# Logit columns as stationary weights in layer 1, six buffers for the softmax rows, a later flag transpose, and one product on VectorE: one change to a four-layer graph kernel

## The chip, the cores and the metric

The kernel runs on one core of a Trainium2 chip. The metric is the device time of one execution in microseconds (us). Each kernel is timed in several executions, and the median counts. A separate execution is recorded by the hardware profiler, and everything said of single instructions comes from that one.

## What is computed

`x` holds 2708 nodes of 256 features and `adj` is a 2708 x 2708 weighted adjacency matrix, which is non-negative in these inputs. Four layers follow one another, each with a residual and a layer norm:

```
x = _layernorm(x + _L0_gnn_ref(x, adj, L0_gnn_W), axis=-1)
x = _layernorm(x + _L1_gnn_ref(x, adj, L1_gnn_W, L1_gnn_a, L1_gnn_gamma, L1_gnn_beta), axis=-1)
x = _layernorm(x + _L2_gnn_ref(x, adj, adj, ...), axis=-1)
x = _layernorm(x + _L3_gnn_ref(x, adj, L3_gnn_neigh_W, L3_gnn_lin_W), axis=-1)
```

Layer 0 is `A @ (x * W)`. Layer 1 is graph attention with 4 heads of 64 features, and a layer norm of its own. Layer 2 needs a sum over neighbours that goes through a GRU cell (the "edge" cell), and graph attention with K = 3 heads, whose logits start from one column per head for every node, `u = x @ (gat_W[k] @ gat_a[k])`; its result goes through a second GRU cell (the "node" cell). Layer 3 is `adj @ h / degree` and a projection.

## The kernel before

**Tiles.** The nodes are 22 tiles of 128 (the last has 20). They are put in six groups (`spans`) of 4, 4, 4, 4, 3 and 3 tiles, and layer 1 works on two groups at a time: `for g in range(0, len(spans), 2)` at L801 gives g = 0, 2 and 4, 8 tiles, 8 tiles and 6.

**Layer 1.** For each g there are two passes (q = 0 and 1), one for each pair of heads. A pass runs over the 22 source tiles c in blocks of two: VectorE builds the unnormalised attention `p` (L855), TensorE multiplies it into `acc` (`heads`, L831: weights 64 columns wide, two products beside each other in the array) and into the sums `den` (`totals`, L841: weights 32 columns wide, four beside each other). The f32 products are recorded as two matmuls each ("passes" of a product below; x counts in the profile count them).

**What is woven in.** `step(c)` at L809 runs after each source tile. It ends the 8 tiles of the previous g in four pairs: `layer1_end` (L697) turns the sums, divides, applies layer 1's norm and the outer norm; `layer1_logits` (L762) then turns the finished `xs` (L770), copies the result into `turn` (L772), writes it to DRAM (L780), and multiplies it with `uw`, the three columns `gat_W[k] @ gat_a[k]`: here the 128 x 128 piece of x is the stationary operand and `uw` the moving one, 3 columns wide (L788). ScalarE copies the 3 columns of both tiles to `u_all` (L792). The pairs of g = 4 have no later pass to hide in; they are run in `while turns` (L907 to L913), between pieces of `raw_sums` (`next(ahead)`).

**The outer norm.** Its last step (L757, L758) is on ScalarE: the negative mean times the reciprocal deviation `rs2`, then a scaled copy into `xs`. `rs2` is a power taken by GpSimd (`power`, L694).

**raw_sums and seven.** `raw_sums` (L365) computes the neighbour sums for the edge cell in six stretches r, each of 11 steps c. A step loads four blocks of `adj_t` (`pa`, issued on SP, L275), clears the own block on GpSimd (L286), forms three sums on VectorE and changes one block in place (L315 to L318), and feeds seven products (L328): the first two use the loaded blocks as they are, the others the sums.

**The logits and the softmax rows of layer 2.** After all pairs are done, `u_all` is split into three bf16 parts (L920) and multiplied with the mask (L932). Later each node has two numbers per head (`st`: a shift and a reciprocal). L1054 to L1071 turn them into rows: six transposes into `ps_t` (L1060), a ScalarE copy into `sr` (L1064), which has two buffers, and DMAs on GpSimd's queue into `st_d` (L1070).

**The flag.** `most` (L1075) is the largest negative part of `adj` per partition. It is turned by TensorE (L1077), reduced to one number (L1079) and made an integer (L1081), which selects a slow path at the very end when an entry is negative. The transpose takes a PSUM tile of the pool `ps_t`; after that the pools are closed (L1117), and the edge cells `gru_t` (L1084) take the same banks as `ps_g`.

**The edge cells.** L1126 to L1139: for each r, the x columns are loaded (SP, L257), the raw sums are run to one stretch ahead, and for r below 4 `gru_t` does 24 gate products (L1097), evacuated by ScalarE (L1102, L1111) and finished on VectorE (L1109 to L1115). The main loop of layer 2 (L1358) starts behind this; `load_stats` (L1160, SP, DMA at L1166) reads the softmax rows of its first unit, ScalarE makes p from them (L1369, L1372) and VectorE multiplies by the blocks (L1373).

**What sets the order.** The program gives a priority by the order in which it is written; a scheduler then orders each engine's instructions by when their inputs are expected. [...]A change in one place can move instructions of other lines past each other.

Of the kernel before, what the change touches and what calls it, by code (L numbers as in the profile page):

```python
# [19 lines left out]
P = 128  # L20
# [7 lines left out]
def kernel(  # L28
# [351 lines left out]
                edges.append(y)  # L380
            yield

    uw = const.tile([P, FC, K], F32, name="uw")

    lwn_d = dram.tile([P, FC, 2 * F], F32, name="lwn_d")

# [22 lines left out]
    if True:  # L409
# [12 lines left out]
        if True:  # L422
# [252 lines left out]
            if True:  # L675
# [21 lines left out]
                def layer1_end(pool, pair):  # L697
# [56 lines left out]
                    for i, (t, s, sums, dens, row) in enumerate(pair):  # L754
                        n = sz(t)
                        o = turn[:, row * F : (row + 1) * F]
                        nc.scalar.mul(mean2[:n, i : i + 1], mean2[:n, i : i + 1], rs2[:n, i : i + 1])  # L757
# [4 lines left out]
                def layer1_logits(pair, apart=1):  # L762

                    pt = ps_t.tile([P, 4, P], F32, tag="tr", name="tr")
                    at = (2 * GT + 1 + 2 * (pair[0][-1] // 2 % 2)) * F
                    xt = turn[:, at : at + 2 * F].rearrange("p (i f n) -> p i f n", i=2, f=FC)
                    for i, a in enumerate(pair):
                        t, n = a[0], sz(a[0])
                        for f in range(FC):
                            nc.tensor.transpose(pt[:, i * FC + f, :n], xs[t][:n, f * P : (f + 1) * P], ident[:n, :n])  # L770
                    if all(sz(a[0]) == P for a in pair):
                        nc.scalar.copy(xt.rearrange("p i f n -> p (i f) n"), pt)  # L772
                    else:
                        for i, a in enumerate(pair):
                            n = sz(a[0])
                            nc.scalar.copy(xt[:, i, :, :n], pt[:, i * FC : (i + 1) * FC, :n])
                    for i, a in enumerate(pair):
                        t, n = a[0], sz(a[0])
                        at, _, d = [p for p in xt_d if p[0] <= t * P][-1]
                        nc.gpsimd.dma_start(d[:, :, t * P - at : t * P - at + n], xt[:, i, :, :n])  # L780
                    for _ in range(apart):
                        yield

                    pm = ps_t.tile([P, 4, P], F32, tag="tr", name="pm")
                    for i, a in enumerate(pair):
                        n = sz(a[0])
                        for f in range(FC):
                            nc.tensor.matmul(  # L788
                                pm[:n, i, :K], xt[:, i, f, :n], uw[:, f, :], start=(f == 0), stop=(f == FC - 1)
                            )  # L790
# [7 lines left out]
                ended = []  # L798

                dens = [keepr.tile([P, W], F32, name=f"den{s}") for s in range(2)]  # L800
                for g in range(0, len(spans), 2):  # L801
# [7 lines left out]
                    def step(c):  # L809
                        with tc.issue_after(product.ins) if g == 0 else nullcontext():  # L810
                            for s in list(steps):
                                if next(s, s) is s:
                                    steps.remove(s)

                        if q == 0 and c % 5 == 1 and len(halves) < len(ended):
                            halves.append(layer1_end(l1, ended[len(halves)]))
                            next(halves[-1])
                            steps.append(itertools.islice(halves[-1], 2))

                        if q == 1 and c % 5 == 0 and c // 5 < len(halves):  # L820
                            steps.append(itertools.chain(halves[c // 5], [None], layer1_logits(ended[c // 5], 1 + (g + 2 >= len(spans)))))
                            next(steps[-1])

                    for q in range(H // 2):
# [82 lines left out]
                while turns:  # L907
                    for a in turns[: k + 1]:
                        if next(a, a) is a:
                            turns.remove(a)  # L910
                            k -= 1
                    next(ahead)
                    k += 1  # L913

                u_parts = sums_pool.tile([P, NT, CT], BF16, name="u_parts", bufs=1)
# [135 lines left out]
                drows = tail.tile([NT, P], F32, name="drows", bufs=1)  # L1051
                nc.scalar.copy(drows, pt[:NT, 0, :])
                nc.gpsimd.dma_start(diag_d, drows)
                for lo in range(0, NT, 4):  # L1054
                    hi = min(lo + 4, NT)
                    at, w = lo * P, width(lo, hi)
                    pt = ps_t.tile([P, 4, P], F32, tag="tr", name="pst")
                    for t in range(lo, hi):
                        n = sz(t)
                        nc.tensor.transpose(  # L1060
                            pt[: 2 * K, t - lo, :n], st[:n, t].rearrange("p i k -> p (i k)"), ident[:n, :n]
                        )
                    sr = tail.tile([2 * K, W], F32, tag="sr", name="sr")
                    nc.scalar.copy(sr[:, :w], pt.rearrange("p t n -> p (t n)")[: 2 * K, :w])  # L1064
                    for u, (a, uw_) in enumerate(units):
                        for h in range(2):
                            c0, c1 = max(at, h * NH + a), min(at + w, h * NH + a + uw_)
                            if c0 < c1:
                                off = c0 - h * NH - a
                                nc.gpsimd.dma_start(st_d[u][:, h, off : off + c1 - c0], sr[:, c0 - at : c1 - at])  # L1070
                    next(ahead)  # L1071
# [7 lines left out]
            nc.vector.tensor_reduce(one, pt[:1, 0, :], AX.X, ALU.max)  # L1079
# [41 lines left out]
    with pool("e_in") as e_in, pool("e_work") as ework, pool("ps_g", 4, space=PSUM, side="right") as ps_g:  # L1121
# [4 lines left out]
        for r, (a, w) in enumerate(raws):  # L1126
# [621 lines left out]
```

## Time and profile before

| what | us |
| --- | --- |
| median of 3 runs | 1837.92 |
| lowest, highest | 1837.21, 1839.69 |
| the profiled execution | 1839.03 |
| its span, first to last instruction | 1837.3 |
| TensorE matmuls busy | 1818.2 |
| VectorE busy | 1265.9 |
| ScalarE busy | 699.5 |
| GpSimd busy | 294.6 |

The mean granted clock of TensorE is 0.999. In the profile, PE is TensorE's matmuls, PEld its weight loads, DVE VectorE, ACT ScalarE, POOL GpSimd and SP SyncE; SPq or ACTq is an engine's queue of DMA issues. A line of the timeline gives the start, the length, the engine, the line of the kernel, the operation, what is written and read, the number of merged instructions (x), and in brackets how long the engine had been idle and what ended that. Layer 0 lasts to about 242 us, layer 1's passes to about 578, the `while turns` stretch to about 617, the softmax rows and the flag to about 694, the edge cells to about 870; the rest is layer 2's main loop and layer 3.

### The profile page before, as it was taken

How to read it: one execution, taken by the hardware profiler on the slowest of the kernel's cores; microseconds unless marked ns; L12 is line 12 of the kernel's file. 1: busy time of each engine (PE TensorE's matmuls, PEld its weight loads, DVE VectorE, ACT ScalarE, POOL GpSimd, SP SyncE). 2: the span in 40 equal slices, each digit the busy share in tenths (PEclk: the TensorE clock that was granted, in tenths of full speed). 3: DMA queues.
4: the chain of work that ended last, by engine and by line, in shares of the span. 5: the costliest groups of instructions: out<-in, count | busy, mean ns of one | idle time of the engine just before them, and what ended most of it. 6: DMA issues, size and time to landing. Idle time of an engine off the chain costs nothing.

```text
span 1837.3 us, 23072 instructions
## 1 busy us (share of the span) xinstructions
PE 1818.2 (99%) x7512; PEld 1037.5 (56%) x7512; DVE 1265.9 (69%) x2242; ACT 699.5 (38%) x1449; POOL 294.6 (16%) x441
## 2 busy tenths in 40 slices
PE   9999999999999999999999999999999999999998
PEld 7888842233446886888444444444445556655556
DVE  5333399999797656554658888686887768945664
ACT  3444420023145114111555655555654656321011
POOL 1322221011113501000002000110300202021211
PEclk9999999999999999999999999999999999999999
DMA  9343310000113567654657666453555445634764
GB/s 303 116 157 138 127 54 25 24 1 21 33 28 95 125 159 189 169 133 106 177 140 203 183 170 173 125 151 110 169 161 129 120 114 142 181 90 122 205 168 134
DMA packets 435710, 237.32 MB, mean 129 GB/s; under 512 B 184460, under 2 KB 422445, under 8 KB 433149
## 3 DMA queue, kind: packets, MB, share of 16 engines
q1 hardware_dynamic: 423534, 210.76, 42.1%
q0 software_dynamic: 7696, 20.50, 3.4%
q10 hardware_dynamic: 4350, 4.50, 0.7%
q8 instruction: 62, 1.02, 0.2%
q14 instruction: 68, 0.55, 0.1%
HBM read 223.00 MB, written 12.66 MB: 128 GB/s over the span
## 4 chain that ended last, share of the span: by engine, by line
PE 89%; DMA 4%; ACT 2%; issue 1%; DVE 1%; SPq 1%; POOL 1%; POOLq 0%; DVEq 0%; ACTq 0%
PE m L328 41%; PE acc L831 11%; PE acc L214 8%; PE bank L1228 8%; PE den L841 6%; PE bank L1204 3%; PE gate L1097 3%; PE bank L1271 2%; PE acc L528 2%; PE pm L434 1%; DMA strip<-in_adj_t_dram 1%; PE m L1475 1%; PE pq L1018 1%; SPq L275 1%; ACT p L1369 1%
## 5 line engine op out<-in xcount | busy, mean ns | idle before, releaser
L855 DVE SCALAR_TENSOR_TENSOR p<-fall,rise,mask 128x1024 f32<-128x1024 f32 (+1 forms) x264 | 288.9, 1154 | 24.3 <-PE den L841 17.0
L1369 ACT ACTIVATE p<-st,e_neg 128x1024 f32<-128x1024 f32 (+1 forms) x198 | 197.4, 1040 | 194.2 <-PE m L328 188.4
L328 PE MATMUL m<-s,xq 128*128 128x512 f32 (+3 forms) x660 | 230.2, 467 | 0.0
L831 PE MATMUL acc<-p,h 128*64 128x512 f32 (+2 forms) x1056 | 209.2, 546 | 0.0
L214 PE MATMUL acc<-turn,strip 128*128 128x257 f32 x792 | 182.7, 381 | 0.9 <-DMA strip<-in_adj_t_dram 0.7
L315 DVE TENSOR_TENSOR s<-p 128x512 f32<-128x512 f32 (+3 forms) x132 | 81.2, 616 | 148.6 <-PE m L328 112.8
L328 PE MATMUL m<-p,xq 128*128 128x512 f32 (+1 forms) x396 | 183.0, 544 | 0.1
L1372 ACT ACTIVATE p<-p 128x1024 f32<-128x1024 f32 (+1 forms) x198 | 178.9, 943 | 0.2
L328 PE MATMUL m<-p,x 128*128 128x512 f32 (+1 forms) x396 | 167.7, 542 | 0.3 <-DVE supt L345 0.3
L328 PEld LDWEIGHTS m<-s,xq 128*128 128x128 f32 x660 | 124.3, 190 | 76.3 <-issue 59.5
L1373 DVE TENSOR_TENSOR p<-p,blk 128x1024 f32<-128x1024 f32 (+1 forms) x132 | 143.0, 1103 | 29.0 <-ACT p L1372 12.5
L214 PEld LDWEIGHTS acc<-turn,strip 128*128 128x128 f32 x792 | 147.2, 189 | 23.1 <-DMA strip<-in_adj_t_dram 2.7
L831 PEld LDWEIGHTS acc<-p,h 128*64 128x64 f32 x1056 | 72.1, 137 | 128.4 <-issue 120.7
L328 PE MATMUL m<-s,x 128*128 128x512 f32 (+3 forms) x330 | 127.2, 467 | 0.0
L328 PEld LDWEIGHTS m<-p,xq 128*128 128x128 f32 x396 | 74.6, 190 | 76.9 <-issue 61.3
L328 PEld LDWEIGHTS m<-p,x 128*128 128x128 f32 x396 | 74.9, 190 | 75.4 <-issue 60.9
L466 DVE TENSOR_SCALAR mask<-strip 128x2816 fp8e4<-128x2816 f32 (+5 forms) x40 | 39.0, 1003 | 110.3 <-DMA strip<-in_adj_t_dram 110.1
L841 PE MATMUL den<-p,h 128*32 128x512 f32 (+2 forms) x1056 | 110.4, 546 | 0.0
L286 POOL TENSOR_TENSOR blk<-blk,offdiag 128x128 f32<-128x128 f32 (+3 forms) x50 | 30.0, 605 | 357.2 <-DMA blk<-in_adj_t_dram 313.4
L481 ACT ACTIVATE below<-strip 128x384 bf16<-128x384 f32 x132 | 78.3, 594 | 18.1 <-DMA strip<-in_adj_t_dram 14.7
L328 PEld LDWEIGHTS m<-s,x 128*128 128x128 f32 x330 | 62.0, 190 | 39.2 <-issue 34.6
L316 DVE TENSOR_TENSOR p<-p 128x512 f32<-128x512 f32 (+3 forms) x132 | 81.6, 618 | 2.4
(295 smaller groups left out, 2647.1 us busy)
## 6 DMA issues: line engine op xcount, KB each, us to landing
strip<-in_adj_t_dram SPq DMA_DIRECT2D x19, 1408.0 KB, 6.1
blk<-in_adj_t_dram SPq DMA_DIRECT2D x88, 256.0 KB, 3.5
blk<-in_adj_t_dram SPq DMA_DIRECT2D x88, 192.0 KB, 4.1
turn<-in_adj_t_dram SPq DMA_DIRECT2D x44, 256.0 KB, 3.2
pa<-in_adj_t_dram SPq DMA_DIRECT2D x88, 128.0 KB, 2.6
blk<-in_adj_t_dram SPq DMA_DIRECT2D x88, 128.0 KB, 2.5
p<-in_adj_t_dram SPq DMA_DIRECT2D x88, 128.0 KB, 2.7
turn<-in_adj_t_dram SPq DMA_DIRECT2D x44, 192.0 KB, 3.2
```

The costliest lines, as they stand in the source:

```text
L214: at = nc.tensor.matmul(acc, s[:, c, :n], rhs(c), start=(c == 0), stop=(c == NT - 1))
L315: nc.vector.tensor_tensor(s1, a21, a22, ALU.add)
L316: nc.vector.tensor_tensor(a21, a21, a11, ALU.subtract)
L328: nc.tensor.matmul(dst[:, :w], lt, rt, start=start and not (one_bank and i in (3, 4, 6)), stop=stop and not (one_bank and i in (1, 2, 5)))
L481: nc.scalar.activation(below[:, : (hi - lo) * P], s[:, lo:hi].rearrange("p c n -> p (c n)"), AF.Relu, scale=-1.0, accum_out=negative[:, BE ...
L831: at = nc.tensor.matmul(acc[s][i * HD : (i + 1) * HD, :ws], hs[c][:, 2 * q + i, :HD], ps[i][:, p0 : p0 + ws], **flags,)
L841: at = nc.tensor.matmul(den[j : j + CT, :ws], hs[c][:, 2 * q + i, HD + 1 - CT :], ps[i][:, p0 : p0 + ws], **flags,)
L855: nc.vector.scalar_tensor_tensor(p[:, :w], fall_b[:, i, :w], rise[:, c, 2 * q + i : 2 * q + i + 1], mask[:, c, at : at + w], ALU.max, ALU. ...
L1228: nc.tensor.matmul(g[:, :w], lt, rt, start=(q == 0), stop=(q == len(terms) - 1))
L1369: nc.scalar.activation(p[:, :, :w], st_k[:, :, :w], AF.Relu, scale=-1.0, bias=e_neg[:, at, k : k + 1])
L1372: nc.scalar.activation(p[:, :, :w], p[:, :, :w], AF.Exp, scale=-1.0)
L1373: nc.vector.tensor_tensor(p[:, :, :w], p[:, :, :w], blk[:, i, :, :w], ALU.mult)
```

## The change

Five edits:

1. `uw` becomes 32 columns wide, filled with zeros beyond the three. In g = 2 and 4 the pairs' logits take `uw` as the stationary operand and the turned x of both tiles as the moving one, 256 columns, so that pair number `slot` writes 32 partitions of its own; ScalarE copies those 32 x 256 numbers to a row of `turn`. When all four pairs are done, `logit_rows` turns the 128 x 256 block back with two transposes and copies it to `u_all` in one instruction. It runs at c = 3 of the next g's first pass, or, for the last, behind the first `next(ahead)` in `while turns`. The pairs of g = 4 keep the old form.
2. In g = 4 the fourth pair's products come one step sooner than the other three.
3. For the last pair the product of mean and `rs2` is on VectorE instead of ScalarE.
4. The six softmax rows are copied into six buffers: the four `sum` tiles and two `den` tiles of layer 1 in place of two of the pool `tail`.
5. The flag's transpose, reduction and comparison stand behind the first edge cell's `gru_t` and use a bank of `ps_g`.

```diff
-    uw = const.tile([P, FC, K], F32, name="uw")
+    uw = const.tile([P, FC, CT], F32, name="uw")
+    nc.gpsimd.memset(uw, 0.0)
...
-                        nc.scalar.mul(mean2[:n, i : i + 1], mean2[:n, i : i + 1], rs2[:n, i : i + 1])
+                        if pair[-1][0] == NT - 1:
+                            nc.vector.tensor_tensor(mean2[:n, i : i + 1], mean2[:n, i : i + 1], rs2[:n, i : i + 1], ALU.mult)
+                        else:
+                            nc.scalar.mul(mean2[:n, i : i + 1], mean2[:n, i : i + 1], rs2[:n, i : i + 1])
...
                     pm = ps_t.tile([P, 4, P], F32, tag="tr", name="pm")
+                    if slot is not None:
+                        rows = slice(slot * CT, (slot + 1) * CT)
+                        at = (14 + pair[0][0] // (2 * GT) % 2) * F
+                        lines = turn[:, at : at + 2 * P].rearrange("p (i n) -> p i n", i=2)
+                        for f in range(FC):
+                            nc.tensor.matmul(
+                                pm[rows, :2], uw[:, f], xt[:, :, f, :], start=(f == 0), stop=(f == FC - 1)
+                            )
+                        nc.scalar.copy(lines[rows], pm[rows, :2])
+                        if slot + 1 == len(pairs):
+                            pending.append(pairs)
+                        return
...
+                def logit_rows(pairs):
+
+                    full, t = len(pairs) * CT, pairs[0][0][0]
+                    at = (14 + t // (2 * GT) % 2) * F
+                    pt = ps_t.tile([P, 4, P], F32, tag="tr", name="pu")
+                    for i in range(2):
+                        nc.tensor.transpose(pt[:, i, :full], turn[:full, at + i * P : at + (i + 1) * P], ident[:full, :full])
+                    nc.scalar.copy(
+                        u_all[:, t : t + 2 * len(pairs)].rearrange("p (j i) k -> p i j k", i=2),
+                        pt[:, :2, :full].rearrange("p i (j s) -> p i j s", s=CT)[:, :, :, :K],
+                    )
...
+                        if q == 0 and c == 3 and pending:
+                            logit_rows(pending.pop())
...
-layer1_logits(ended[c // 5], 1 + (g + 2 >= len(spans)))))
+layer1_logits(ended[c // 5], 1 + (g + 2 >= len(spans) and c < 15), c // 5, ended)))
...
                     next(ahead)
+                    if pending:
+                        logit_rows(pending.pop())
...
+                rows = [keepr.tile([P, W], F32, tag=f"sum{i // 2}{i % 2}", name="sr") for i in range(4)] + dens
...
-                    sr = tail.tile([2 * K, W], F32, tag="sr", name="sr")
+                    sr = rows.pop(0)[: 2 * K]
...
-            pt = ps_t.tile([P, 4, P], F32, tag="tr", name="pl")
-            nc.tensor.transpose(pt[:1, 0, :], most, ident)
-            one = const.tile([1, 1], F32, name="one")
-            nc.vector.tensor_reduce(one, pt[:1, 0, :], AX.X, ALU.max)
-            signed = const.tile([1, 1], I32, name="signed")
-            nc.vector.tensor_scalar(signed, one, 0.0, None, ALU.is_gt)
...
                 gru_t(ps_g, ework, yt, edges[r], xt, 2 * w, wih, whh, b_edge)
+                if r == 0:
+                    pt = ps_g.tile([P, W], F32, tag="gate", name="pl")
+                    nc.tensor.transpose(pt[:1, :P], most, ident)
+                    one = const.tile([1, 1], F32, name="one")
+                    nc.vector.tensor_reduce(one, pt[:1, :P], AX.X, ALU.max)
+                    signed = const.tile([1, 1], I32, name="signed")
+                    nc.vector.tensor_scalar(signed, one, 0.0, None, ALU.is_gt)
```

The order of the instructions, laid beside that of before, changes as follows. TensorE: only the lists named above, and two products of `raw_sums` (L328) that stood between the flag's transpose and the first gate product come behind the gate products of the first edge cell and the flag. SP: the x columns of the second edge cell come nine issues sooner, and the load of the first softmax rows (L1166) comes behind 21 more issues for `pa`. ScalarE: the first p of layer 2 (L1369) comes behind the first four evacuations of the first edge cell instead of ahead of them. VectorE: the second step of `raw_sums` behind the softmax rows comes wholly ahead of the first p product (L1373), and ahead of the third step there are two p products instead of four, and two half-width sums of p (L315 to L318) instead of seven. In the passes of g = 4 small instructions of ScalarE and VectorE (L685 to L748) change places among each other.

More of the change, by code (lines that the diff above doesn't have):

```diff
@@ L760, in layer1_end, with layer1_logits @@
                         )
-                def layer1_logits(pair, apart=1):
+                def layer1_logits(pair, apart=1, slot=None, pairs=()):
                     pt = ps_t.tile([P, 4, P], F32, tag="tr", name="tr")
@@ L788, in layer1_logits @@
                             nc.tensor.matmul(
-                                pm[:n, i, :K], xt[:, i, f, :n], uw[:, f, :], start=(f == 0), stop=(f == FC - 1)
+                                pm[:n, i, :K], xt[:, i, f, :n], uw[:, f, :K], start=(f == 0), stop=(f == FC - 1)
                             )
@@ L796, in layer1_logits @@
                             nc.scalar.copy(u_all[:n, a[0]], pm[:n, i, :K])
-                ended = []
+                def logit_rows(pairs):
[8 more added lines that the diff above has]
+                    )
+                ended, pending = [], []
                 dens = [keepr.tile([P, W], F32, name=f"den{s}") for s in range(2)]
@@ L820, in step @@
                         if q == 1 and c % 5 == 0 and c // 5 < len(halves):
-                            steps.append(itertools.chain(halves[c // 5], [None], layer1_logits(ended[c // 5], 1 + (g + 2 >= len(spans)))))
+                            steps.append(itertools.chain(halves[c // 5], [None], layer1_logits(ended[c // 5], 1 + (g + 2 >= len(spans) and c < 15), c // 5, ended)))
                             next(steps[-1])
```

## Prediction

> **What bounds the kernel now.** I read the page's part 1 and chain first, then the busy time of each engine in stretches of 10 us, then the timeline wherever TensorE falls short of 10.
>
> ```profile
> PE 1818.2 (99%) x7512; PEld 1037.5 (56%) x7512; DVE 1265.9 (69%) x2242; ACT 699.5 (38%) x1449; POOL 294.6 (16%) x441
> ...
> PE 89%; DMA 4%; ACT 2%; issue 1%; DVE 1%; SPq 1%; POOL 1%; POOLq 0%; DVEq 0%; ACTq 0%
> ```
>
> TensorE is the bound; only what shortens its list or closes one of its gaps counts. The span has 1837.3 - 1818.2 = 19.1 us of gaps, and the change can reach few of them. Near an edited line TensorE falls short in three places: by 0.98 us in 600 to 610, by 0.88 in 690 to 700, and by 0.67 and 0.33 in 710 to 720 and 720 to 730, where VectorE is busy 9.97 and 9.52 of 10. The first, in the timeline:
>
> ```profile
> 599.30 7.51 POOL L694 TENSOR_TENSOR o_rs<-o_var,neg_half 128x1 f32<-128x1 f32 x2 [1.82 <-DVE o_var L693]
> ...
> 606.84 0.29 ACT L757 ACTIVATE o_mean<-o_mean,o_rs 20x1 f32<-20x1 f32 x1 [5.43 <-POOL o_rs L694]
> ...
> 608.28 1.05 PE L788 MATMUL pm<-uw,turn 128*128 128x3 f32 x8 [0.90 <-ACT turn L772]
> ```
>
> The two powers take 7.51 us on GpSimd and end at 606.81, 0.41 us after VectorE, which runs sums of `raw_sums` without a break, falls idle at 606.40 (L317, 606.02 and 0.38 long). ScalarE is held behind L757, then L758 and the copy L772 follow, and TensorE stands 0.90 us. The second gap:
>
> ```profile
> 695.01 0.27 DVE L1079 TENSOR_REDUCE one<-pl 1x1 f32<-1x128 f32 x1
> ...
> 695.34 1.78 PE L1097 MATMUL gate<-xt,whh 128*128 128x452 f32 x4 [0.88 <-DVE one L1079]
> ```
>
> The flag's transpose is at 693.42. The first gate wants its PSUM bank, and the reader L1079 is queued on VectorE behind four sums. The third starts in SP's queue of issues:
>
> ```profile
> 684.02 4.01 SPq L275 DMA_DIRECT2D pa<-in_adj_t_dram  x5
> 691.16 0.34 SPq L1166 DMA_DIRECT2D st<-st  x1
> ...
> 696.99 8.07 SPq L275 DMA_DIRECT2D pa<-in_adj_t_dram  x16
> ```
>
> and goes on in the timeline:
>
> ```profile
> 701.59 0.40 DVE L315 TENSOR_TENSOR s<-pa 128x226 f32<-128x226 f32 x1 [6.14 <-DMA pa<-in_adj_t_dram]
> ...
> 719.82 0.30 PEld L328 LDWEIGHTS m<-pa,xq 128*128 128x128 f32 x2 [1.02 <-DVE pa L316]
> ...
> 723.31 0.30 PEld L328 LDWEIGHTS m<-pa,xq 128*128 128x128 f32 x2 [0.68 <-DVE pa L316]
> ```
>
> SP holds at L1166 from 688.03 to 691.16 and again before 696.99; SP's list of waits puts 3.0 and 1.4 us of this on "DMA st<-sr", the row DMAs that themselves wait for two buffers in turn. So VectorE has nothing for 6.14 us, and is overfull from 712 to 724, where TensorE waits for it. Finally the logits:
>
> ```profile
> 446.73 1.05 PE L788 MATMUL pm<-uw,turn 128*128 128x3 f32 x8
> ...
> 447.72 2.35 PE L841 MATMUL den<-p,h 128*32 128x512 f32 x20
> ```
>
> **What the Trainium skill says.** "SBUF — State Buffer", section "Who interferes with whom": a VectorE tensor_tensor with both inputs in SBUF contends with GpSimd's reads for one port pair, and the second to issue is wholly blocked. The trace agrees: the power ends 0.41 us after VectorE falls idle. "TensorE: Matmul & The Clock Gate", section "Part 3: Packing small matmuls — row/col tiling": products in different 32-column tiles run beside each other. The trace agrees: the 1056 passes of L841 are busy 110.4 us, 0.105 each, though none streams fewer than 320 columns. The new logits are alone in their tile, so all that this could give them is an overlap with the totals behind them.
>
> **The change, part by part** (negative is a gain, in us).
>
> *Logits of 8 pairs.* Removed: 8 passes per pair, from 446.73 to 447.72, 0.99. Added: two products of 256 columns, two passes each, in the same column tile, so one behind the other. A column costs 18.20 us / 48 passes / 452 = 0.839 ns (the 48 gate passes in the chain), so 4 x 256 x 0.839 ns = 0.86, and I allow 0.04 for a first weight load not wholly hidden (it is 0.106 in L655). 0.90 - 0.99 = -0.09, times 8 = -0.7. The block's return: 2 x 2 transposes at 0.59/4 = 0.15 (four L770 take from 544.53 to 545.12), +0.6. Together -0.1. Bounds: if the following totals overlap half of it, 0.45 per pair, -4.3 + 0.6 = -3.7; if each pass costs its whole recorded latency (0.380, L655), 1.52 per pair, +4.2 + 0.6 = +4.8. L655's 44 passes take 2.4 us, 11 in each of four tiles at 0.22: they pipeline, which is why I stay at 0.86. ScalarE's copies grow from 0.15 to about 0.36 (the 128x257 copy at L665), 8 x 0.2, beside passes in which it is busy 2 to 6 of 10 us: nothing; uncovered they would be 1.7. The `uw` fill is at the start, where TensorE waits 3.4 us for data: nothing, at most 0.3. One step less for the fourth pair: its products stay at the same place in TensorE's list, nothing.
>
> *Mean product.* ScalarE loses two of 0.29. VectorE gets two instructions (0.13 to 0.15 each, by L693), and they wait for the power: queued behind are L316 and L317 of the next step. In the list they stand behind the L315 that ends at 605.59. There VectorE stops, which frees the port: the power should end near 605.59 + 0.41 = 606.0 instead of 606.81. L758 then starts about 606.3 instead of 607.17, L772 about 0.9 sooner, and the gap of 0.90 closes. The sums held back come about 606.4 to 607.6; TensorE asks for them at 608.8 and later. Value -0.8; at best -1.2 (the 0.58 gap at 596 too), at worst +0.6 if the power takes its time whatever VectorE does (VectorE then stands from 605.59 to 606.85).
>
> *Flag.* The gates start without it: -0.88. It comes behind 48 gate passes, 0.15 of TensorE as before. New waits: its bank must have been read by ScalarE (g_r of the second half). ScalarE has L1369 ahead of that, which waits for L1166's load. SP issues that behind 21 more `pa`: 21 x 0.5 from about 689 gives 699.5, landed by 704 (4.16 from issue to L1369 before). g_r is read near 706, the flag wants it at 693.4 + 18.2 = 711.6: 5 us of cover. Value -0.9, between -0.9 and +1.
>
> *Six buffers.* No TensorE wait names the rows, so directly nothing. But SP's 3.0 and 1.4 us vanish, `pa` lands some 6 us sooner, and VectorE does that step at 695 instead of 701.6. From 713.64 to the next gates at 725.33 TensorE has 10 + 3 x 14 = 52 passes of 0.191 (29.41/154), 9.93, and takes 11.69: stalls of 1.76. Ahead of the third step VectorE now has two p products fewer (2 x 1.22) and five half-width sums fewer (5 x 0.67), 5.8 less. ScalarE's later start pushes r's tanh to about 714.8, and the third step's L316 to about 717.2, when TensorE wants it at 718.0: no stall. The fourth step's L318 ends near 722.4 against 722.1: 0.3 and more remain. I take 0.8 of 1.76: -1.0, between -1.76 and +1.0. What is late next is this L318. The later first p costs nothing: its user is the main loop at 870.
>
> Sum: -0.1 - 0.8 - 0.9 - 1.0 = -2.8. The profiled execution, 1839.03 (span 1837.3 and 1.7 around it), becomes 1836.2; it lies 1.1 over the median, so the median goes from 1837.92 to 1835.1.
>
> **Rivals.** *A: all gaps close.* Stalls of 1.76 and 1.2 go whole, the logits gain 0.15 a pair: -1.2 + 0.6 - 1.2 - 0.9 - 1.76 = -4.5, 1833.4; with half an overlap at the logits -7.5, 1830.4. For it: VectorE's 6 idle us come just ahead of its overfull stretch. Against: same-tile passes can't overlap each other. *B: the gain is taken back.* A stall that goes returns later, since SP's list is delayed and at 880 to 890 DMA is busy 1.02 while TensorE waits; only the flag's 0.9 stays: 1837.0. Against: from 725 to 867 TensorE has no gap, so it keeps a lead. *C: slower.* The narrow products don't pipeline in their tile: 1.52 a pair, +4.8 in place of -0.1, 4.8 - 2.7 = +2.1, 1840.0. It decides from (0.99 x 8 + 2.7 - 0.6)/8 = 1.25 us a pair. For it: the recorded latency. Against: L655.
>
> **How the numbers follow.** Forecast 0.56 (1833.3 to 1836.7), A 0.18, B 0.16, C 0.10. About 0.2%, 3.7 us, is what a measurement can tell from no change: below 1834.24 is faster, above 1841.6 slower. Faster: a quarter of the forecast and all but a little of A, plus some chance that reordered lists do more than I count: 0.35. Slower: half of C and an unseen hold in a list: 0.08. Same: 0.57. The range of 8 in 10 reaches from a little under the middle of A's two times to a little short of C's time: 1831.5 to 1839.5.
>
> **What would show it.** Right: L788's successors take 0.9 us a pair from their start to the next totals; the power at 600 ends near 606.0 and no gap of 0.9 follows; the first gate follows `raw_sums` without a gap; SP issues `pa` from 684 to 699 without 3 us holes, and 719 to 725 has under 1 us of waits. Wrong: pairs at 0.5 or 1.5 us; a wait of TensorE at the flag; a VectorE wait at the new product that shows up in TensorE; a new gap at 870 to 930.

## The result, and the profile after

| kernel | median, us | runs | ratio to before | 95% interval |
| --- | --- | --- | --- | --- |
| before | 1839.81 | 18 | | |
| after | 1837.04 | 18 | 0.9984 | 0.9977 to 0.9991 |
| after, timed again later (e9) | 1835.17 | 19 | 0.9976 | 0.9969 to 0.9983 |

The change makes the kernel faster by 0.16%, or 0.24% in the second set: 2.9 us (1.7 to 4.2) and 4.4 us (3.1 to 5.7). The forecast was a gain of 2.8. The kernel before had moved, from 1837.92 in the first three runs to 1839.81, so the forecast is compared as a difference; as a plain time, 1837.04 lies in the prediction's range of 1831.5 to 1839.5 and 0.3 above the band of the forecast itself. Both intervals exclude no change, though the first gain is below the 3.7 us that the prediction took as the least that can be told from it. The two sets of one kernel also show that sets differ by some 1.5 us; below, kernels less than that apart are told apart by their traces, not by their times.

The profiled execution of after has a span of 1834.4 us, 2.9 below before. Its page, busy time and chain:

```profile
PE 1817.6 (99%) x7484; PEld 1034.7 (56%) x7484; DVE 1267.5 (69%) x2244; ACT 700.5 (38%) x1449; POOL 297.7 (16%) x442
...
PE 93%; DMA 3%; SPq 1%; DVE 1%; ACT 1%; issue 1%; POOL 0%; POOLq 0%; DVEq 0%
```

TensorE has 28 matmuls fewer, is busy 0.6 us less and holds 93% of the chain instead of 89%: the gain is in gaps. The mean product (edit 3), in the timeline of after:

```profile
599.54 4.95 POOL L695 TENSOR_TENSOR o_rs<-o_var,neg_half 128x1 f32<-128x1 f32 x2 [1.81 <-DVE o_var L694]
...
604.02 0.16 DVE L759 TENSOR_TENSOR o_mean<-o_mean,o_rs 128x1 f32<-128x1 f32 x1 [0.45 <-POOL o_rs L695]
...
604.53 0.15 DVE L759 TENSOR_TENSOR o_mean<-o_mean,o_rs 20x1 f32<-20x1 f32 x1 [0.35 <-POOL o_rs L695]
...
607.50 0.95 PE L804 MATMUL pm<-uw,turn 128*128 128x3 f32 x8
```

VectorE stops at 603.57, 0.45 us before its first product; it gets the second 0.35 us after the end of the first. The two powers end at 604.49, after 4.95 us instead of 7.51, and the matmuls that had waited 0.90 us follow without a gap. The gates, the flag and the fourth step, TensorE's matmuls and then its weight loads:

```profile
692.32 1.68 PE L1124 MATMUL gate<-xt,whh 128*128 128x452 f32 x4
...
710.52 0.27 PE L1167 MATMUL pl<-ident,most 128*1 128x128 f32 x1
```

```profile
720.98 0.30 PEld L328 LDWEIGHTS m<-s,x 128*128 128x128 f32 x2 [0.23 <-DVE s L318]
```

The first gate follows `raw_sums` without a wait, the flag's transpose waits for nothing, and of the stalls from 713 to 725 one of 0.23 us is left, at the L318 of the fourth step, where the prediction put the next late thing. The reason that the stalls are gone is SP's queue, in the timeline of after:

```profile
687.37 12.95 SPq L275 DMA_DIRECT2D pa<-in_adj_t_dram  x24
700.48 0.34 SPq L1200 DMA_DIRECT2D st<-st  x1
```

24 issues of `pa` in one piece, where before had 5, a hold, 5, a hold, and 16. Then a gap that is new, busy times from 880 to 890 and the timeline (the columns of the first are the stretch, its length, and busy time and count for PE, PEld, DVE, ACT and POOL, then clock, DMA share and GB/s; before has TensorE busy for 9.55 us of this stretch):

```profile
880.00:890.00 10.00, 8.37 (x21) 3.63 (x20) 2.46 (x3) 3.81 (x6) 0.81 (x2) 1.00 1.13 311
```

```profile
866.43 0.33 ACTq L379 DMA_DIRECT2D sup<-supt  x1
871.52 0.89 SPq L1229 DMA_DIRECT2D wk<-in_L_gnn_gat_W_dram  x2
...
883.13 1.75 PE L1262 MATMUL bank<-xt,whh 128*128 128x452 f32 x4 [1.63 <-DMA xt<-xt]
```

In before, the same instruction:

```profile
885.37 1.75 PE L1228 MATMUL bank<-xt,whh 128*128 128x452 f32 x4 [0.45 <-DMA xt<-xt]
```

The x columns of the first edge cell in the main loop are late: a wait of 1.63 us where before had 0.45. SP starts on the loads behind it (`wk`, two weight matrices, then `xt`) once the store of `sup` at 866.43 has landed (866.43 + 5.0 is 871.43); in the code, the pool of `wk` is opened where that of `supt` was closed. That store takes 5.0 us from issue to landing in after and 2.7 in before:

```profile
q8 instruction: 1, 0.02, 1.8%
...
sup<-supt ACTq DMA_DIRECT2D x1, 448.0 KB, 5.0
```

This is the DMA view of 866 to 872 us of after (packets, MB, share of 16 engines; KB and us to landing). The same stretch of before has no packet of that queue, and:

```profile
sup<-supt ACTq DMA_DIRECT2D x1, 448.0 KB, 2.7
```

In after, one 16 KB packet of the queue "instruction" took 1.8% of 16 engines for 6 us, that is 1.74 us of one engine; the trace has it start at 867.8, in the middle of the store. In before the nearest such packets are at 858.8 and 897.9.

**Stage by stage.** The lead is the start of a matmul in the kernel before less the start of the same matmul in another kernel. Its growth over a stretch is what the stretch gained (median over 25 neighbouring matmuls, us). Stretches by the times of before: layer 0 to 243, the passes with the logits to 604, the mean product to 609, softmax rows, flag and first cell to 713.7, the stalls to 726, then to the first `xt` product at 886, and on to 1700.

| kernel | layer 0 | logits | mean | flag | stalls | to xt | rest |
| --- | --- | --- | --- | --- | --- | --- | --- |
| after | -0.74 | 0.46 | 1.16 | 1.37 | 1.61 | -1.63 | 0.39 |
| e9 after again | -0.07 | 0.47 | 1.17 | 1.37 | 1.76 | -0.81 | 0.70 |
| e1 logits alone | 1.05 | 0.44 | 0.26 | 1.29 | -1.89 | -1.38 | 0.19 |
| e2 rows alone | 0.09 | 0.00 | 0.00 | 1.01 | 1.76 | -0.40 | 0.20 |
| e5 flag alone | -0.39 | 0.00 | 0.00 | 1.37 | -0.58 | 0.68 | 0.27 |
| e6 mean alone | -0.53 | 0.00 | 1.17 | 0.10 | -0.07 | 0.69 | 0.44 |
| e12 rows, mean | 0.15 | 0.01 | 1.17 | 1.08 | 1.76 | 0.48 | -0.05 |
| e3 no logits | -0.10 | 0.01 | 1.16 | 1.18 | 1.75 | 0.13 | 0.17 |
| e7 e3 and fill | -1.14 | -0.02 | 1.17 | 1.19 | 1.75 | 0.51 | 0.45 |
| e8 shift by 2 | -2.58 | 0.46 | 1.17 | 1.27 | 1.75 | 0.36 | -0.10 |
| e11 shift by 10 | -2.62 | 0.47 | 1.17 | 1.32 | 1.75 | 0.69 | 0.24 |
| e4 shift by 18 | 0.06 | 0.44 | 1.17 | 1.36 | 1.75 | 0.41 | 0.19 |
| e10 shift by 26 | -1.03 | 0.44 | 1.17 | 1.21 | 1.75 | -0.42 | 0.24 |

Four columns repeat within 0.2 us wherever the same edits are in. Layer 0, whose code is touched only by the fill of `uw` and, in e4, e8, e10 and e11, by some small transposes at its start, scatters by 3.7 us. It differs by 0.67 between two profiles of one kernel. Of after's -1.63, 0.4 is lost near 767 already and 1.2 at the `xt` product.

### The profile page after: what moved, and what is told of

Same layout as the page of the kernel before. It is cut to its first block, busy times and chain, and to the rows that moved or that the text cites. A ratio compares the mean times of both kernels' runs of the same rounds, so it can differ in the third digit from the quotient of the medians.

```text
span 1834.4 us, 23008 instructions
## 1 busy us (share of the span) xinstructions
PE 1817.6 (99%) x7484; PEld 1034.7 (56%) x7484; DVE 1267.5 (69%) x2244; ACT 700.5 (38%) x1449; POOL 297.7 (16%) x442
## 3 DMA queue, kind: packets, MB, share of 16 engines
q8 instruction: 62, 1.02, 0.2%
## 4 chain that ended last, share of the span: by engine, by line
PE 93%; DMA 3%; SPq 1%; DVE 1%; ACT 1%; issue 1%; POOL 0%; POOLq 0%; DVEq 0%
PE m L328 42%; PE acc L862 11%; PE acc L214 8%; PE bank L1262 8%; PE den L872 6%; PE gate L1124 4%; PE bank L1238 3%; PE bank L1305 2%; PE acc L529 2%; PE pm L435 1%; PE m L1509 1%; SPq L275 1%; PE pq L1051 1%; DMA strip<-in_adj_t_dram 1%; DMA p<-in_adj_t_dram 1%
## 5 line engine op out<-in xcount | busy, mean ns | idle before, releaser
L328 PE MATMUL m<-s,xq 128*128 128x512 f32 (+3 forms) x660 | 230.0, 466 | 0.0
L315 DVE TENSOR_TENSOR s<-p 128x512 f32<-128x512 f32 (+3 forms) x132 | 82.0, 622 | 146.8 <-PE m L328 105.1
L328 PE MATMUL m<-p,xq 128*128 128x512 f32 (+1 forms) x396 | 182.9, 544 | 0.1
L328 PE MATMUL m<-p,x 128*128 128x512 f32 (+1 forms) x396 | 167.7, 542 | 0.3 <-DVE supt L345 0.3
L328 PEld LDWEIGHTS m<-s,xq 128*128 128x128 f32 x660 | 124.4, 190 | 76.2 <-issue 59.2
L328 PE MATMUL m<-s,x 128*128 128x512 f32 (+3 forms) x330 | 127.1, 467 | 0.0
L328 PEld LDWEIGHTS m<-p,xq 128*128 128x128 f32 x396 | 74.6, 190 | 76.9 <-issue 61.1
L328 PEld LDWEIGHTS m<-p,x 128*128 128x128 f32 x396 | 74.8, 190 | 75.5 <-issue 60.7
L328 PEld LDWEIGHTS m<-s,x 128*128 128x128 f32 x330 | 62.0, 190 | 39.2 <-issue 34.8
```

The lines of the kernel that those rows point to most:

```text
L315: nc.vector.tensor_tensor(s1, a21, a22, ALU.add)
L328: nc.tensor.matmul(dst[:, :w], lt, rt, start=start and not (one_bank and i in (3, 4, 6)), stop=stop and not (one_bank and i in (1, 2, 5)))
```

## The experiments

"Before" is the kernel before and "after" the whole changed kernel.

**e1: the logits edit alone**

```diff
+    nc.gpsimd.memset(uw, 0.0)
...
+                            nc.tensor.matmul(
+                                pm[rows, :2], uw[:, f], xt[:, :, f, :], start=(f == 0), stop=(f == FC - 1)
+                            )
...
+                            logit_rows(pending.pop())
```

> The kernel before with the logits edit alone (weights 32 columns wide, two returns; rows, flag and mean product as before). Theory T1: the eight pairs and the two returns together give about 0.3 us on TensorE (the lead of the changed kernel over the one before grew from -0.73 to -0.39 across them), and, because TensorE's list is 28 passes shorter, a 16 KB instruction fetch of TensorE falls on the store of sup and delays it by 2 us, so that the first xt product of the edge cell behind the main loop's start waits about 1 us longer than the 0.45 of the kernel before: the time is +0.5 us, between 0 and +1.2. Rival T2: the wait for xt grew in the changed kernel only because TensorE came 3.4 us earlier to loads that the DMA engines could not bring sooner; then this kernel, which comes no earlier, keeps a wait of 0.5 and its time is -0.3 us. Rival T3: the lead of -0.73 at the end of layer 0 belongs to the edit (the fill of uw on GpSimd); then the first products are 0.2 to 1.1 us late here too and are not late in kernels without the fill.

Ratio 1.0003 (0.9994 to 1.0012), +0.6 us. T1 has its parts: 0.44 from the logits, an instruction packet of 1.75 us at 870.0, a store of 5.0 us and a wait of 1.83 us for `xt`. That its time of +0.5 was met is in part luck: the profiled execution is 1.0 us shorter than that of before, 1.05 of it from layer 0. T2 is not settled here, since the kernel comes to this product 1.15 us earlier than before, where T2 supposed that it comes no earlier. But SP starts on `wk` 1.2 us later than in before (873.76 against 872.60), although the store was issued 1.15 us sooner. T3 falls: the first products are not late. Unforeseen are 1.29 us at the flag, which was not moved, and the loss of 1.89 us behind it, in the weight loads of e1:

```profile
718.66 0.30 PEld L328 LDWEIGHTS m<-pa,xq 128*128 128x128 f32 x2 [2.91 <-DVE pa L316]
```

What TensorE had won by 692 it lost at the third step, whose sums still wait for SP's held loads. The flag's transpose stands where it stood in TensorE's list, but the first gate, at 692.40, does not wait for its reader, which starts at 694.10. So the logits edit alone closes the flag's gap; that another turn of the PSUM buffers gave the gate another bank is only argued.

**e2: six row buffers alone**

```diff
-                    sr = tail.tile([2 * K, W], F32, tag="sr", name="sr")
+                    sr = rows.pop(0)[: 2 * K]
```

> The kernel before with the six buffers for the softmax rows alone. Theory T1: SP's two holds go, the first two row sums of the stretch behind the rows are done 6 us earlier, and TensorE's stalls between 713 and 725 of the kernel before (1.76 us) fall to about 0.2: -1.5 us by the second edge cell; TensorE's list is as long as before, its instruction fetch stays near 858 and away from the store of sup, and nothing is given back at 880: -1.5 us in the end, wait for xt about 0.5. Rival T2 (loads behind 870 bound by the DMA engines): 1.0 to 1.3 of it comes back as a wait for xt, -0.3 us in the end. Rival R: the stalls only close when the flag is out of the way as well; then they stay above 1 us here and the time is the same as before.

Ratio 0.9979 (0.9972 to 0.9985), -3.9 us: more than either theory. The stalls go whole (1.76) with the flag still in its place, so rival R falls, and 1.01 us of the flag's gap goes as well, in the timeline of e2:

```profile
693.18 0.27 PE L1078 MATMUL pl<-ident,most 128*1 128x128 f32 x1
...
693.91 0.27 DVE L1080 TENSOR_REDUCE one<-pl 1x1 f32<-1x128 f32 x1
...
694.23 0.30 PEld L1098 LDWEIGHTS gate<-xt,whh 128*128 128x128 f32 x2 [0.37 <-DVE one L1080]
```

The reader L1080 follows 0.73 us behind the transpose instead of 1.59, because the sums it is queued behind got their `pa` 1.1 us sooner and are done. So the row buffers and the flag's move close the same gap. The wait for `xt` is 0.85, with a store of 2.8.

**e5: the flag's move alone**

```diff
-            pt = ps_t.tile([P, 4, P], F32, tag="tr", name="pl")
...
+                    pt = ps_g.tile([P, W], F32, tag="gate", name="pl")
```

> The kernel before with the flag's move alone. As the prediction had it, it is worth -0.9 us by itself. Theory I (the flag's gap and the row buffers overlap): TensorE gains 0.9 us or so at the first gate, arrives that much sooner at the third step of the stretch behind the rows, whose sums still wait for SP's held loads, and loses it there: the stalls from 713 to 725 grow from 1.76 to about 2.6, and the time is that of the kernel before, between -0.4 and +0.2 us. Rival, the prediction's sum: the stalls stay at 1.76, -0.9 us.

Ratio 1.0004 (0.9996 to 1.0012). No gain is measured; -0.9 us lies just outside the interval. The trace: 1.37 us won at the gate, 0.58 of it lost in the stalls, in the weight loads of e5:

```profile
719.75 0.30 PEld L328 LDWEIGHTS m<-pa,xq 128*128 128x128 f32 x2 [1.93 <-DVE pa L316]
```

Before waits 1.02 us there. Theory I has the mechanism and overstates it: 0.79 us is left at 726, not nothing.

**e12: rows and mean product, the flag where it was**

```diff
-                    sr = tail.tile([2 * K, W], F32, tag="sr", name="sr")
+                    sr = rows.pop(0)[: 2 * K]
...
+                            nc.vector.tensor_tensor(mean2[:n, i : i + 1], mean2[:n, i : i + 1], rs2[:n, i : i + 1], ALU.mult)
```

> The kernel before with six row buffers and the mean product on VectorE, the flag where it was: the kernel without the logits edit less the flag's move. From the row buffers alone (a flag wait of 0.37 us left on TensorE's weights, where the kernel before had 1.23, and a lead of 2.6 us gained from 608 to 725) the flag's move on top of the buffers is worth 0.3 us: this kernel gains 2.5 us or so between 608 and 725, and its time is 0.3 above the kernel without the logits edit, about -5.5. The prediction's sum would make it 0.9 above.

Ratio 0.9974 (0.9965 to 0.9983), -4.8 us. The time does not separate it from e3, the trace does: from 609 to 726 it gains 1.08 + 1.76 = 2.84, e3 1.18 + 1.75 = 2.93. With the buffers in place the flag's move is worth 0.1 us, less than either expected and within the 0.2 by which the flag column scatters.

**e6: the mean product alone**

```diff
+                            nc.vector.tensor_tensor(mean2[:n, i : i + 1], mean2[:n, i : i + 1], rs2[:n, i : i + 1], ALU.mult)
```

> The kernel before with the product of mean and reciprocal deviation on VectorE for the last pair, nothing else. The prediction had -0.8 us; in the kernel without the logits edit TensorE's lead grew by 1.23 us at the first old-form logits. Theory: the gap of 0.90 closes and the power ends near 604.5; TensorE is 0.9 to 1.2 us ahead at 608, the chain of the softmax rows shifts with it, so the lead stays through 725: -1.0 us. Rival: the lead is lost at 713 to 725, where the sums wait for SP's held loads: 0.0.

Ratio 1.0000 (0.9992 to 1.0008): 1 us can't be seen in it, nor 0.0 told from it. The trace decides: 1.17 us won, -0.07 in the stalls, so the lead stays, as the theory had it.

**e3: the change without the logits edit**

```diff
-                    if slot is not None:
...
-                            logit_rows(pending.pop())
```

All pairs have the old form.

> The changed kernel without the logits edit (rows, flag and mean product changed). Theory T1: mean -1.0, flag -1.1, rows -1.6, nothing back at 880 since the instruction fetch stays away from the store of sup: -3.7 us against the kernel before, that is 0.8 less than the changed kernel, wait for xt about 0.5. Rival T2: TensorE comes 3.7 us early to loads that can't come sooner, the wait for xt is 1.6 or more and the time is about -2.5 us.

Ratio 0.9967 (0.9955 to 0.9979), -6.1 us (3.9 to 8.3), more than the 3.7 of T1; the gain in the trace is 4.5 (span 1832.8). The timeline of e3 at the place in question:

```profile
865.84 0.33 ACTq L379 DMA_DIRECT2D sup<-supt  x1
...
868.57 1.40 SPq L1199 DMA_DIRECT2D wk<-in_L_gnn_gat_W_dram  x3
...
881.24 1.00 PE L1232 MATMUL bank<-xt,whh 128*128 128x452 f32 x2 [0.32 <-issue]
```

TensorE starts this product 1.9 us earlier than in after, behind a wait of 0.32 instead of 1.63. T2, loads that can't come sooner, is refuted: here they come sooner. The instruction packet is at 854.7.

**e4, e8, e11, e10: after with 18, 2, 10 and 26 small transposes at the start**

```diff
+                    shift = ps_t.tile([P, 4, P], F32, tag="tr", name="shift")
+                    for i in range(18):
+                        nc.tensor.transpose(shift[:32, i % 4, :32], ident[:32, :32], ident[:32, :32])
```

> The whole changed kernel, and 18 transposes of 32x32 pieces of the identity ahead of the first product, where TensorE waits for data. Nothing reads them. They put 36 more weight loads and matmuls into TensorE's list, so every later instruction fetch of TensorE comes about 3.4 us earlier in relation to the work. Theory T1: the fetch that took 1.74 us at 867.8 on one DMA engine comes at about 864.4, ahead of the store of sup; the store lands in 2.7 us instead of 5.0, the wait for xt falls from 1.63 to about 0.3, and the time is 1.2 us below the changed kernel's, -4.1 against the kernel before. Rival T2: the wait stays 1.6 and the time is that of the changed kernel, -2.9.

> The changed kernel with 2 instead of 18 of the small unread transposes at the start, so 4 more weight loads and matmuls in TensorE's list in place of 36. Theory T1 (the store of sup is held by an instruction fetch): the fetch moves by less than half a microsecond and still falls within the store's 1.6 us near 867; the store takes 4 to 5 us, the first xt product waits 1.2 to 1.7, and the time is the changed kernel's, -2.9. Should the fetch fall elsewhere, the wait is under 0.6 and the time near that with 18. Rival W: the 18 transposes helped by something else than where the fetch falls (TensorE busy before the data is there); then these 2 have part of it and the wait for xt shrinks while fetch and store still meet.

> The changed kernel with 10 of the small unread transposes, 20 more weight loads and matmuls in TensorE's list. With 2 the fetch came at 868.5, with 18 at 855.4, so this one is between: theory T1 says that if it comes between 866 and 869 the store takes 3.5 to 5 us and the time is near -2.9; if it comes before 865, the store takes 2.7 to 2.9, there is no wait for xt over 0.5, and the time is -4.5 to -6.

> The changed kernel with 26 of the small unread transposes at the start instead of 18. Theory T1: 52 more weight loads and matmuls in TensorE's list; the fetch is ahead of the store, as with 18 (it was at 855.4 there), the store takes 2.7 to 2.9, no wait for xt over 0.5, and the time is 1.5 to 3 us below the changed kernel's: -4.5 to -6 against the kernel before. Rival W2 (the number 18 was lucky in layer 0): the store and the wait as in T1, but the time is within 1 us of the changed kernel's, since layer 0 decides.

Together with after itself once more, unaltered:

> The changed kernel a second time, nothing altered. Theory T1: where an instruction fetch falls is set by TensorE's list, so the fetch meets the store of sup here too (a fetch within 866 to 870 us), the store lands later than 3 us after its issue, and TensorE waits 1 us or more for the first xt product; -2.9 us. Rival C (chance of one execution): the fetch is elsewhere, or the store takes 2.7 and the wait is under 0.5. For layer 0: its waits for strips, which differed by 2 us between kernels that share its code, are expected to differ between these two looks at one kernel as well.

| kernel | ratio (95%) | packet at, us long | store, us | wait for xt | weight loads idle |
| --- | --- | --- | --- | --- | --- |
| after | 0.9984 (0.9977 to 0.9991) | 867.8, 1.74 | 5.0 | 1.63 | 2.43 |
| e9 | 0.9976 (0.9969 to 0.9983) | 865.7, 0.88 | 3.4 | 1.25 | 2.05 |
| e8, 2 | 0.9986 (0.9979 to 0.9994) | 868.5, 0.88 | 3.5 | none | 0.73 |
| e11, 10 | 0.9976 (0.9968 to 0.9985) | 859.2 | 2.7 | none | 0.24 |
| e4, 18 | 0.9967 (0.9956 to 0.9979) | 855.4 | 2.9 | none | 0.85 |
| e10, 26 | 0.9971 (0.9960 to 0.9981) | 855.5 | 2.8 | 0.48 | 1.28 |

The wait is that on the matmul's row; the last column is the idle time on the weight loads' row at the same product, 1.25 in before and 0.24 between neighbouring weight loads that wait for nothing there.

The DMA view of e9 from 862 to 872, and the matmul that waits:

```profile
q8 instruction: 1, 0.02, 0.6%
...
sup<-supt ACTq DMA_DIRECT2D x1, 448.0 KB, 3.4
```

```profile
881.48 1.75 PE L1262 MATMUL bank<-xt,whh 128*128 128x452 f32 x4 [1.25 <-DMA xt<-xt]
```

and of e4, 858 to 872, with no packet of that queue behind 855.4:

```profile
sup<-supt ACTq DMA_DIRECT2D x1, 448.0 KB, 2.9
```

```profile
880.18 1.75 PE L1265 MATMUL bank<-xt,whh 128*128 128x452 f32 x4
```

And of e8, where the store is late and TensorE does not wait, the matmul and its weight load:

```profile
882.93 1.75 PE L1265 MATMUL bank<-xt,whh 128*128 128x452 f32 x4
```

```profile
882.90 0.30 PEld L1265 LDWEIGHTS bank<-xt,whh 128*128 128x128 f32 x2 [0.73 <-issue]
```

The packet falls on the store in four profiles (after, e9, e1, e8): 5.0, 3.4, 5.0 and 3.5 us to landing. It falls elsewhere in the other ten: 2.6 to 2.9. Where the packet is 0.88 us long the store is 0.7 to 0.8 later than the 2.7 of before, and where it is 1.74 or 1.75, 2.3. That much is shown. For e9, T1 holds for store and wait (its packet lies 0.3 us ahead of the stretch that T1 named) and rival C falls. "DMA: Bandwidth & Descriptors" in the Trainium skill, section "Queues, rings and completion order", says that each DMA engine goes round its queues a whole packet at a time, and its section "Why a DMA increments its semaphore by 16 and not by 1" that all the data has landed only when every engine it runs on has counted. The trace agrees as far as it goes, for it does not name the engine of a packet: in after all but nine of the store's 144 packets end by 868.93, and those nine end one after the other from 869.89 to 871.00, behind the instruction packet, which ends at 869.5.

From the late store to TensorE is one step more, and it isn't sure: three of the four wait 1.25 to 1.83, but e8 not at all, against T1's 1.2 to 1.7 (its store is also faster than T1's 4 to 5 us), and e2 waits 0.85 with a store of 2.8. Where TensorE waits, the loads took 11.6 to 13.0 us from the first `wk` to the first `xt` product; in e8 11.5 was enough. What sets how fast these loads run in one execution stays open. The packet also moved further than T1 of e4 had it: 10 to 12 us with 18 transposes instead of 3.4; why stays open too. Rival W, that the 18 helped in another way, isn't excluded: for e8 it had that the wait shrinks while packet and store still meet, and so it came. Against it, e3, e7 and e12 have no transposes and wait 0.32 us or less. The times don't decide: e4 and e10 measure 6.1 and 5.3 us below before, e11 4.4 (T1 had 4.5 to 6), e8 2.6, and the profiles of e8 and e11 lost 2.6 us in layer 0. Rival W2 of e10, that the time stays within 1 us of after's, is not excluded either, since e9, which is after once more, measures 4.4. The intervals of e4 and e9 overlap, so that e4 beats after is shown in the trace (1.2 to 1.6 us at the `xt` product) and not by the times.

**e7: e3, and `uw` filled all the same**

```diff
-    uw = const.tile([P, FC, K], F32, name="uw")
+    uw_ = const.tile([P, FC, CT], F32, name="uw")
+    nc.gpsimd.memset(uw_, 0.0)
+    uw = uw_[:, :, :K]
```

> The kernel without the logits edit (rows, flag and mean product changed), and uw all the same 32 columns wide and filled with zeros on GpSimd; its old form reads the first three columns. In the three profiles without the fill TensorE waits 0.50 to 0.82 us for a strip of adj_t at 118 us; in the three with it, not at all. Theory F: the fill, one more instruction at the head of GpSimd's list and a shift of what lies behind uw in SBUF, moves the loads that run beside this strip, and the wait is gone here too: 0.7 us less than the kernel without the fill, -6.8 us against the kernel before where that one measured -6.1. Rival: the six waits differ by chance, and one of 0.5 to 0.8 is here; the time is the same as without the fill.

Theory F is right on the wait and wrong on the time. At 118 us the six kernels without the fill wait 0.26 to 0.90 us for a strip, the eight with it less than 0.2. But the ratio is 0.9967 (0.9955 to 0.9979), that of e3, and another strip is late, in the matmuls of e7:

```profile
219.01 1.14 PE L214 MATMUL acc<-turn,strip 128*128 128x257 f32 x4 [1.16 <-DMA strip<-in_adj_t_dram]
```

Layer 0 waits for one strip or another in nearly every profile (in e11 1.89 us at 163); the fill decides what happens at 118, and no gain of it shows in the time.

## Why the prediction was right, and where it was not

The forecast of -2.8 was met by -2.9 and -4.4, but by terms that were all too small and a loss that it had given to a rival. That they cancelled is luck; the mechanism of each gap was mostly right, the sizes and the way they add up were not.

*Logits, -0.1: measured -0.45.* The chain of four passes takes 0.9 us in its tile, as the prediction had it. The totals' timeline in after shows what it left out:

```profile
490.84 0.40 PE L794 MATMUL pm<-turn,uw 128*32 128x256 f32 x1
490.85 0.46 PE L872 MATMUL den<-p,h 128*32 128x320 f32 x2
491.08 0.38 PE L794 MATMUL pm<-turn,uw 128*32 128x256 f32 x1
```

The totals of other column tiles start 0.01 us behind the first pass and ahead of the second. This is so at four of the eight pairs (447, 461, 490 and 549 us); at the other four the product behind starts 0.96 us or more after the first pass. Over the four pairs of g = 2 the lead grows by 0.68, 0.17 a pair and not 0.09. The first return costs 0.51 instead of 0.3. It stands between totals that run beside each other; the second, ahead of other transposes, takes 0.22. Why the first costs more is not shown. The pairs of g = 4 and the second return together give 0.28. The bounds held, and rival C (1.52 a pair) is refuted.

*Mean product, -0.8: measured -1.17.* Three things were mis-sized. The prediction had both powers done 0.41 us behind VectorE's stop; the second ends 0.92 us behind it, and VectorE waits for each in turn (0.45 and 0.35). But VectorE stops at 603.57, two us sooner than I read from the list. And the gap's price is not the 0.90 on the matmul's row. The weight-load row of before has the same wait:

```profile
608.28 0.86 PEld L788 LDWEIGHTS pm<-uw,turn 128*128 128x128 f32 x7 [1.25 <-ACT turn L772]
```

"Perfetto Trace Analysis" in the Trainium skill, section "Tensor Engine Instruction (MATMUL, LD_WEIGHTS)", says that a matmul's end is worked out from its size and not observed. Recorded ends overlap the next start here (0.35 long at 0.19 apart), so idle time on a matmul's row leaves out the overlap. The weight load's 1.25 is near the 1.17 that came back.

*Flag, -0.9: alone -1.37 at the gate, 0.79 of it left at 726, and 0.1 beside the row buffers.* The same reading error, 0.88 on the matmul's row and 1.23 on the weight load's in before:

```profile
695.34 0.30 PEld L1097 LDWEIGHTS gate<-xt,whh 128*128 128x128 f32 x2 [1.23 <-DVE one L1079]
```

The larger error is in the form of the sum: the flag's reader was queued behind sums that the row buffers speed up, and without the buffers what the flag gains is partly lost at the third step. Edits that end in one wait were priced as if they stood apart: the flag's move, the row buffers and even the logits edit each close most or all of this gap alone (1.37, 1.01 and 1.29), so the 1.37 in after can't be put down to the flag's move. The cover of 5 us for the bank held: no wait at 710.52.

*Six buffers, -1.0: alone -2.77 by 726 (1.01 + 1.76).* The stalls were read rightly, from starts and counts, as 1.76 us; I left 0.8 of it to a late L318 of the fourth step, which turned out as 0.23 on the weight loads of after and as at most 0.15 in the lead. The pair of edits gives 2.93 where the prediction had 1.9.

*Nothing given back from 725 on:* wrong, and the new gap that the prediction named as a sign of it came. 1.2 us comes back at the first `xt` product in after and 0.8 in e9. Rival B had the place and the DMA engines; its reason, that the loads can't come sooner, is refuted by e3, e12 and e4, which reach the product 0.6 to 1.3 us earlier than after (start less wait) and wait 0.32 us or less (0.77 to 1.12 on the weight loads' row, below the 1.25 of before). What goes before the loss is the store held by an instruction packet, from which SP's loads and the late product follow in after, e9 and e1. The logits edit put the packet there, by making TensorE's list shorter: no kernel without that edit has it there, and 10 or more transposes move it away. That a late store alone makes TensorE wait is not shown, since e8 has one and loses nothing.

The sum by the table: 0.45 + 1.17 + 1.37 + 1.75 = 4.7 gained, 0.8 to 1.2 given back, and layer 0 adds or takes a us or more by itself (0.7 lost in after's profile). The number was right because what was missing on both sides happened to be alike. Without the logits edit (e3) the change is worth 6.1 us (3.9 to 8.3) by the times and 4.5 by the trace; that edit gains 0.45 us where it stands and loses 0.8 to 1.4 at another place (after, e9, e1). The times don't prove that the change is better without it: the intervals of e3 and e9 overlap.

## What to carry to other kernels

Price a TensorE gap from start to start, or from the weight loads' row, not from the idle time on a matmul's row. Before adding edits up, ask of each gap which instruction ends it and what that is queued behind: edits that close one gap share one gain. When a gain is smaller than expected far behind the edit, look into the DMA queues for a transfer that took longer than its like, and for what sat on its engine.

## What the runs showed of the hardware

The profile lists a DMA queue named "instruction". Its 16 KB packets are taken to be TensorE's from their number (argued, not shown), 62 of them for 7512 weight loads and as many matmuls in before, some 240 to a packet. Such a packet takes 0.88 to 1.88 us in these profiles. A store of 448 KB that met one landed 0.7 to 2.3 us later than without. Where the packets fall moves with the length of TensorE's list: with 56 weight loads and matmuls fewer one came 7 to 11 us later (after, e9, e1), and with 36 of them back (e4) 10 to 12 us earlier again. So an edit can delay a transfer at a place that it has nothing to do with, and in after, e9 and e1 TensorE then waited for what was queued behind it.
